# Layer 2's state-space attention: delta's product computed once per group, kept in SBUF, and the stage's instruction order rebuilt

## The chip, the cores and the metric

The kernel runs on one core of a Trainium2 chip. It is one program: five stages, one after the other, four engines that compute (TensorE, here PE; VectorE, DVE; ScalarE, ACT; GpSimd, POOL), each with its own in-order queue, and DMA queues, of which SyncE (SP) issues most. The metric is the device time of one execution in microseconds, median of several runs.

## The reference, cut to what matters

The whole network is eight residual blocks. The change touches the fifth alone, a Mamba layer on the 4096 tokens by 128 features of the activations, seen as sequences of 256 tokens. Two sequences make a group of 512 tokens; there are eight groups.

```python
xz = einsum('bld,ed->bel', hidden_states, in_proj_w)      # 128 -> 512
x, z = xz[:, :256], xz[:, 256:]
x = silu(causal depthwise conv of 4 taps over x, + conv_b)
x_dbl = einsum('bdl,kd->blk', x, x_proj_w)                # 256 -> 8 + 8 + 8
dt_lr, B, C = x_dbl split in 8, 8, 8
dt = einsum('blr,dr->bld', dt_lr, dt_proj_w)              # 8 -> 256
A = -exp(A_log) + low_rank_scale * (U @ V) / sqrt(8)
delta = softplus(dt + dt_proj_b)
def step(h, t):                                           # 256 features, 8 states
    dA = exp(dlt[..., None] * A)
    h = h * dA + (dlt * ut)[..., None] * Bt[:, None, :]
    y = einsum('bdn,bn->bd', h, Ct)
    return (h, y)
_, ys = scan(step, h0, xs)
y = (ys + u * D) * silu(z)
return einsum('bld,md->blm', y, out_proj_w)
```

Softplus is ln(1 + exp(a)). The kernel takes it as max(a, ln(1 + exp(min(a, 40)))), with a = dt + dt_proj_b, so the product dt is needed in two places: under the minimum and under the maximum.

## The kernel before, in words

**One group's way through the stage.** The group's 512 tokens are normalized (POOL, `sln`), transposed on PE and put into `ypad`; PE makes u (four shifted products against the folded convolution weights `wx`, for each of two halves of 128 features) and z; ACT takes them out of PSUM into `su` and applies SiLU. PE makes the joint projection (`ssm_xp`), ACT puts it in `sxs`, and SP sends its B and C rows to DRAM and loads B back spread over all partitions (`sB`, 1 MB each, two for a group) and C as `scc`.

Then comes delta (`ssm_dt`, `ssm_soft`). For each half c, PE multiplies `sxs` by the delta weights (`W("dt")`, in the trace `spb<-sxs,w_L2a`, 80 rows by 512 columns) into one of two PSUM banks `spb`; DVE adds the bias and takes the minimum with 40 into `s4` (in the trace `s<-spb,w_L2a`). ACT runs Exp and Ln over both halves at once (`s<-s`, 128 by 1024). PE then makes the same products a second time, and DVE, in one instruction for each half, adds the bias and takes the maximum with `s4`, into `sdl` (`sdl<-spb,w_L2a,s`). `sdl` is delta.

From delta POOL makes w = delta * u (`sw<-sdl,su`), four products of w with B (`sb<-sw,sB`, 128 by 2048, one for each half and quartet of states; seven buffers) and the spread of C (`scq<-scc,dmask`). ACT makes exp(delta * A) for one half and state at a time (`abuf<-sdl,sA`, three PSUM buffers), and DVE runs the scan (`sb<-abuf,sb`, 128 by 512), 16 of them for a group. PE transposes the scanned states in 16 steps of four into the single PSUM bank `shT`; ACT or DVE copies each out (`shs<-shT`), and PE contracts them with C (`sy<-shs,scq`). At the end ACT takes `sy` out, PE transposes back and adds u * D (`spb<-su,sdd`, `spb<-w_const,s`), DVE multiplies by the gate (`s<-spb,su`), PE applies the output projection (`spb<-w_L2a,s`), and DVE adds the result to the residual `xt`.

**What sets the order.** In this stage nothing is issued as it is written. A recorder (`Recorder`) takes down every operation of all eight groups with a due time: the step's place in a table (`SSM[2]`, entries `dt`, `soft`, `b` and so on, counted in scans), times `slot`, plus a shift for its kind (`shift`). A planner (`Recorder.run`) then goes through all of them with estimated costs, giving each free engine the ready operation with the earliest due time, and the order it finds is what each of PE, DVE, ACT, POOL is given as its queue, in order; SP is ordered too by when its transfers become ready. An operation may be marked as a choice between ACT and DVE (`rec.choice()`); `pen` is what DVE's turn costs in due time, `ahead` how far past the oldest unplanned operation it may look. A DVE operation with two inputs in SBUF, or a tensor_scalar from SBUF to SBUF, is marked `two`, and the planner starts it only when it thinks POOL is free (line 607). All instructions come out of one recording helper, line 301, so the profile tells them apart by tiles only.

**The neighbours.** The stage before is layers 0 and 1; the one behind is the expert layer, whose first loads (`w_moe`, `w_in`) wait for the end of this stage's memory. The table `SSM[4]` and the other uses of `ssm_dt` belong to a later stage with 16 states, which the change leaves as it is.

Of the kernel before, what the change touches and what calls it, by code (L numbers as in the profile page):

```python
# [16 lines left out]
AF = mybir.ActivationFunctionType  # L17
ALU = mybir.AluOpType
# [4 lines left out]
P = 128  # L23
NSEQ = 16
SEQ = 256
NTOK = NSEQ * SEQ
D = 128
GT = 512
# [646 lines left out]
class Ker:  # L675
# [565 lines left out]
    def l1(self, rec, hh, W0, F):  # L1241
# [8 lines left out]
        with ExitStack() as st:  # L1250
# [52 lines left out]
        t=((14.0, 32.0, 50.0), (14.0, 48.0, 84.0)), pen=178.7, ahead=200.0, shift={  # L1303
            "ffn": -11.8, "fin": -58.9, "front": 52.1, "gate": -15.6, "max": 39.6, "mn": -190.3, "pre": -12.5,
            "rec": 42.7, "sc": -35.2, "stick": 0.3, "tail": 116.8, "terms": 21.7, "up": 102.7, "val": 112.6, "w": 347.1,
        },
# [344 lines left out]
    def ssm_dt(self, S, c, last):  # L1651
# [11 lines left out]
        else:  # L1663
            nc.vector.tensor_scalar(ex, b, bias, 40.0, ALU.add, ALU.min)

    def ssm_soft(self, S, k):
        nc, ex, tp = self.nc, S["ex"], self.tp
        if k == 0:
            self.func(ex, ex, AF.Exp)
            self.func(ex, ex, AF.Ln, bias=1.0)  # L1670
        elif k == 1:
            S["w"] = self.ring("sw", [P, 2, GT], 2)
            nc.gpsimd.tensor_tensor(S["w"], S["dl"].rearrange("p c s t -> p c (s t)"), S["u"], ALU.mult)
        else:
            nq, cc = S["N"] // 4, S["cc"]
            cq = S["cq"] = self.ring("scq", [P, nq, 16, 32], 2)
            for q in range(0, nq, 2):
                nc.gpsimd.tensor_tensor(
                    cq[:, q : q + 2].rearrange("p q t j -> p (q t) j"),
                    cc[:, q : q + 2].rearrange("p q t -> p (q t)")[:, :, None].to_broadcast([P, 32, 32]),  # L1680
                    self.dmask[:, None, :].to_broadcast([P, 32, 32]), ALU.mult,
                )
                self.rec.also(S["w"])
# [69 lines left out]
    def ssm_out(self, S):  # L1753
# [10 lines left out]
        if S["res"]:  # L1764
# [11 lines left out]
            silu=-37.5, xp=-33, dt=(-31, -29.5, -25.5, -24), soft=(-28, -22.5, -3), bl=(-17, -9.5, -1.5, 6.5),  # L1776
            b=(-6, -2), ys=(7.2, 11.2), gt=(12, 13), out=16.3, fin=(17, 17.7, 19), slot=1.55, pen=84.3, ahead=127.7, shift={
            "": -125.5, "b": 67.9, "bload": -113.8, "dt": -200.5, "ev": 31.8, "exp": 33.9, "f": 246.7, "gt": -3.9,
            "in": 52.0, "n": -59.0, "out": 61.0, "r": -161.7, "scan": 83.0, "silu": -129.7, "soft": -121.0,
            "src": -425.4, "tr": 59.0, "xp": 3.9, "y": 118.9, "ys": -27.2,  # L1780
        },
# [1 line left out]
        2: dict(  # L1783
            nt=1, nu=4, ln=(-32, -31.5, -30), src=-29.5, u=(-28.7, -26.6), z=(-24.4, -23.4),
            silu=-22, xp=-19, dt=(-17.6, -16.7, -13.3, -12.4), soft=(-15.8, -11, 3), bl=(-17, -9.5),
            b=(-6, -2), ys=(7.2, 11.2), gt=(12, 13), out=17.5, fin=(18, 18.1, 18.2), slot=2.0, pen=111.1, ahead=183.8, shift={
            "": 112.0, "b": -43.4, "bload": -48.9, "dt": -6.2, "ev": -98.7, "exp": 66.6, "f": -14.8, "gt": -12.7,
            "in": -8.9, "n": -4.4, "out": -5.7, "scan": 2.2, "silu": -119.1, "soft": 38.6, "src": -22.5, "stick": 66.3,
            "tr": -56.2, "xp": -50.7, "y": -93.8, "ys": -93.0,
        },  # L1790
        ),
    }
# [1 line left out]
    def ssm_run(self, items, begin, norm, finish, N, after=None):  # L1794

        nq, n = N // 4, len(items)
        L = 8 * nq
        pl = self.plan
        ev = []

        def at(t, f, *a):
            ev.append((t, len(ev), f, a))

        self.rec.shift = {k: pl["slot"] * v for k, v in pl["shift"].items()}

        for i, item in enumerate(items):
            S = dict(N=N)
            o = i * L
            at(o + pl["ln"][0] - 0.01, begin, item, S)
            gens = {}  # L1810

            def step(kind, f, item, S, gens=gens):
                if kind not in gens:
                    gens[kind] = f(item, S)
                next(gens[kind], None)

            for t in pl["ln"]:
                at(o + t, step, "n", norm, item, S)
            at(o + pl["src"], self.ssm_src, S)
            if after:  # L1820
                at(o + pl["src"] + 0.1, after, item)
            for c in range(2):
                at(o + pl["u"][c], self.ssm_in, S, c)
            for k in range(2):
                at(o + pl["z"][k], self.ssm_in, S, 2 + k)
            at(o + pl["silu"], self.ssm_silu, S)
            at(o + pl["xp"], self.ssm_xp, S)
            for k in range(4):
                at(o + pl["dt"][k], self.ssm_dt, S, k % 2, k > 1)
            for k in range(3):  # L1830
                at(o + pl["soft"][k], self.ssm_soft, S, k)
            for q in range(nq):
                s = o + 8 * q
                at(o + pl["bl"][q], self.ssm_bload, S, q)
                for c in range(2):
                    at(s + 4 * c + pl["b"][0], self.ssm_b, S, q, c)
                for j in range(8):
                    at(s + j - 2.6, self.ssm_exp, S, q, j)
                    at(s + j, self.ssm_scan, S, q, j)
                    t = s + 9 + j  # L1840
                    at(t + 0.2, self.ssm_tr, S, q, j)
                    at(t + 0.5, self.ssm_ev, S, q, j)
                    if j % 2:
                        at(t + 1.3, self.ssm_y, S, q, j // 2)
            e = o + L
            for k in range(2):
                at(e + pl["ys"][k], self.ssm_ys, S, k)
                at(e + pl["gt"][k], self.ssm_gt, S, k)
            at(e + pl["out"], self.ssm_out, S)
            for t in pl["fin"]:  # L1850
                at(e + t, step, "f", finish, item, S)
        ev.sort(key=lambda e: e[:2])
        for t, _, f, a in ev:
            self.rec.key, self.rec.kind = pl["slot"] * t, f.__name__[4:] or a[0]
            f(*a)
        self.nc.record(None)
        self.rec.penalty = pl["pen"]
        self.rec.run(pl["ahead"])
        self.last_act = self.nc.scalar.last
# [248 lines left out]
    def l3_ffn(self):  # L2108
        nc = self.nc
        with ExitStack() as st:  # L2110
# [89 lines left out]
        pen=819.1, ahead=200.0, shift={  # L2200
            "aff": -5.1, "gate": -11.4, "gelu": 394.9, "hT": -62.4, "ln": 137.7, "max": -127.7, "mn": -410.9,
            "nrm": 69.1, "qkv": -128.2, "rot": -171.0, "sc": 39.2, "stick": 33.1, "tr": -158.4, "up": 14.7,
            "val": -79.2, "w": 39.8, "w2": 358.8, "wo": -262.4, "x": 1.0, "yT": 26.4,
        },
# [352 lines left out]
```

## Time and profile before

| | us |
|---|---|
| three runs | 3786.04, 3786.32, 3792.03 (median 3786.32) |
| the profiled execution | 3790.45 |
| its span, first to last instruction | 3788.6 |
| mean granted TensorE clock in it | 0.949 |
| this stage: from its first memsets to its last residual add | 871.42 to 1177.95 |
| stages before / behind | 871.42 / 2610.65 |

Over the whole span PE is busy 87%, DVE 83%, ACT 69%, POOL 65%. Within this stage's 306.53 us PE is busy 277.6, DVE 227.6, ACT 215.9 and POOL 198.8, and the granted clock is 0.97. These are sums of execution times that overlap at their edges, so an engine with 90% may have no room left.

Where POOL's eight groups begin says how the stage is paced. The instruction `sw<-sdl,su` starts at 914.8, 937.0, 961.2, 998.8, 1031.5, 1064.8, 1098.4 and 1120.8 us, so the distances are 22, 24, 38, 33, 33, 34 and 22 us: the first groups and the last follow each other closely, those in the middle are far apart.

### The profile page before, as it was taken

Reading aid. Unit: us, or ns where it says so; the run is one execution under the profiler, and the core shown is the slowest. Engines: PE = TensorE matmul, PEld = TensorE weight load, DVE = VectorE, ACT = ScalarE, POOL = GpSimd, SP = SyncE. Lnnn points to the kernel's source line nnn. Section 1 sums busy time; section 2 is a strip of 40 time slices with the busy share of each in tenths; the row PEclk is TensorE's granted clock in tenths of the full one; section 3 lists DMA queues with packets and bytes.
Section 4 is the critical chain, followed back from the end, with each engine's and each line's share of the span. In section 5 each row is a group of like instructions: output and inputs, shape, how many; then the busy total and the mean of one; then the engine's idle time right before and its main releaser. Section 6 shows DMA issues by size and latency. Waiting matters only on the chain.

```text
span 3788.6 us, 77710 instructions
## 1 busy us (share of the span) xinstructions
PE 3302.9 (87%) x31401; PEld 2222.1 (59%) x31401; DVE 3156.3 (83%) x5442; ACT 2621.7 (69%) x4276; POOL 2453.4 (65%) x1174
## 2 busy tenths in 40 slices
PE   6770168887998998799999999999999969999998
PEld 3320145563566887366666666666666647777776
DVE  4999898774886776399999999999999968888874
ACT  5660034545874333599999999999999957777765
POOL 4654323215772001699999999999999978655553
PEclk9995589998999999899999999999999989999999
DMA  1021111101111001322222222222222210000001
GB/s 48 13 38 25 37 51 36 38 21 60 69 69 38 7 6 43 107 91 92 97 97 96 98 98 92 92 97 92 92 92 93 101 60 28 11 13 6 5 18 32
DMA packets 107236, 217.94 MB, mean 58 GB/s; under 512 B 53065, under 2 KB 78284, under 8 KB 87756
## 3 DMA queue, kind: packets, MB, share of 16 engines
q1 hardware_dynamic: 104140, 208.19, 16.6%
q8 instruction: 247, 4.05, 0.5%
q10 hardware_dynamic: 2736, 4.78, 0.4%
q14 instruction: 113, 0.93, 0.1%
HBM read 182.66 MB, written 15.47 MB: 52 GB/s over the span
## 4 chain that ended last, share of the span: by engine, by line
PE 48%; ACT 17%; DVE 4%; issue 2%; POOL 1%; DMA 1%; POOLq 0%; SPq 0%; DVEq 0%; ACTq 0%
PE spb L301 14%; PE fb L301 10%; PE shT L301 8%; ACT abuf L301 5%; ACT shs L301 5%; PE gu L301 5%; PE sy L301 4%; PE md L301 3%; PE fp L301 2%; ACT L301 2%; ACT su L301 2%; ACT s L301 2%; PE mx L301 1%; DVE qr L301 1%; DVE mx L301 1%
## 5 line engine op out<-in xcount | busy, mean ns | idle before, releaser
L301 POOL TENSOR_TENSOR sb<-sw,sB 128x2048 f32<-128x2048 f32 x288 | 1338.6, 4672 | 47.2 <-PE shT L301 46.2
L301 DVE TENSOR_TENSOR_SCAN sb<-abuf,sb 128x512 f32<-128x512 f32 x1152 | 1324.9, 1209 | 43.9 <-ACT abuf L301 22.7
L301 ACT ACTIVATE abuf<-sdl,sA 128x510 f32<-128x510 f32 x1152 | 780.9, 701 | 46.8 <-DVE sb L301 42.9
L301 PEld LDWEIGHTS shT<-w_const,sb 128*128 128x128 f32 x4608 | 594.8, 194 | 284.8 <-ACT shs L301 118.3
L301 PE MATMUL shT<-w_const,sb 128*128 128x128 f32 x4608 | 667.8, 283 | 29.6 <-ACT shs L301 16.0
L301 ACT COPY shs<-shT 128x512 f32<-128x512 f32 x920 | 517.0, 596 | 50.2 <-PE shT L301 36.8
L301 PE MATMUL sy<-shs,scq 128*32 128x256 f32 x4608 | 359.9, 390 | 0.2 <-DVE shs L301 0.2
L301 PE MATMUL spb<-ypad,wx 128*128 128x512 f32 x640 | 305.9, 615 | 6.1 <-ACT su L301 3.0
L301 POOL TENSOR_TENSOR qn<-qn,qr 128x512 f32<-128x512 f32 x128 | 163.7, 1280 | 171.9 <-DVE qr L301 123.5
L301 DVE TENSOR_REDUCE mx<-fp 128x8 f32<-128x1024 f32 x160 | 193.4, 1217 | 20.0 <-PE fp L301 18.7
L301 ACT ACT_TABLE_LOAD x148 | 189.9, 1283 | 25.1 <-PE fb L301 18.3
L301 PEld LDWEIGHTS spb<-ypad,wx 128*128 128x128 f32 x640 | 116.6, 194 | 143.4 <-issue 116.2
L301 PE MATMUL gu<-my,gu 128*128 128x512 f32 x768 | 196.5, 404 | 2.6 <-ACT gu L301 2.2
L301 ACT ACTIVATE mh<-gu,w_moe 128x512 f32<-128x512 f32 x128 | 88.1, 688 | 158.4 <-PE gu L301 136.0
L301 DVE COPY shs<-shT 128x512 f32<-128x512 f32 x232 | 153.4, 685 | 46.6 <-PE shT L301 31.5
L301 PEld LDWEIGHTS sy<-shs,scq 128*32 128x32 f32 x4608 | 100.1, 108 | 113.1 <-issue 44.0
L301 ACT ACTIVATE pt<-fp 128x1024 f32<-128x1024 f32 x96 | 96.4, 1024 | 100.5 <-PE fp L301 93.8
L301 PE MATMUL fb<-wqkv_hi,hT 128*128 128x512 f32 x384 | 161.2, 438 | 4.6 <-ACT mn L301 1.4
L301 PEld LDWEIGHTS gu<-my,gu 128*128 128x128 f32 x768 | 140.3, 190 | 33.3 <-ACT gu L301 2.5
L301 POOL TENSOR_TENSOR yn<-xt,nmv 128x512 f32<-128x512 f32 x21 | 21.9, 1042 | 201.8 <-DVE nmv L301 196.1
L301 PE MATMUL spb<-sxs,w_L3a 80*128 80x512 f32 x256 | 141.2, 633 | 6.0 <-DVE s L301 2.6
L301 POOL TENSOR_TENSOR qn<-qn,nr 128x512 f32<-128x512 f32 x128 | 130.9, 1044 | 19.9 <-ACT nr L301 19.6
(385 smaller groups left out, 7063.5 us busy)
## 6 DMA issues: line engine op xcount, KB each, us to landing
sB<-scr SPq DMA_DIRECT2D x144, 1024.0 KB
QS<-qk SPq DMA_DIRECT2D x48, 128.0 KB
KS<-qk SPq DMA_DIRECT2D x48, 128.0 KB
pks<-pk SPq DMA_DIRECT2D x4, 1152.0 KB
rec<-pks SPq DMA_DIRECT2D x8, 576.0 KB
x<-xt SPq DMA_DIRECT2D x16, 256.0 KB
xo<-x SPq DMA_DIRECT2D x16, 256.0 KB
sb<-in_cw_dram SPq DMA_DIRECT2D x5, 512.0 KB
```

The costliest lines, as they stand in the source:

```text
L301: r = f(*a, **kw)
```

## The change: what it does

For the layer with 8 states (`N == 8`, this stage) the product of a half is made once. It is taken out of PSUM with the bias added, by ACT or DVE as the planner chooses, into `sdl` (`ssm_once`). The minimum with 40 is now one DVE instruction over both halves, from `sdl` into `s4`, at the head of `ssm_soft`; Exp and Ln stay; the maximum is one DVE instruction over both halves, of `sdl` and `s4` into `sdl` (`ssm_pos`). Besides, the entries `pen`, `ahead` and `shift` of this stage's plan have other values, with a new one for the maximum (`pos`), so the planner puts all of the stage in a new order.

```diff
+    def ssm_once(self, S, c):
+
+        nc, W = self.nc, S["W"]
+        if c == 0:
+            S["ex"] = self.ring("s4", [P, 2, GT], 2)
+            S["dl"] = self.ring("sdl", [P, 2, 2, SEQ], 2)
+        bias, dl = W("dtb")[:, c : c + 1], S["dl"].rearrange("p c s t -> p c (s t)")[:, c]
+        b = self.sbank()
+        self.mm(b, W("dt")[0:80, c * P : (c + 1) * P], S["xs"])
+        with self.rec.choice():
+            nc.scalar.activation(dl, b, AF.Identity, bias=bias)
+            nc.vector.tensor_scalar(dl, b, bias, None, ALU.add)
+
+    def ssm_pos(self, S):
+
+        dl = S["dl"].rearrange("p c s t -> p c (s t)")
+        self.nc.vector.tensor_tensor(dl, dl, S["ex"], ALU.max)
+
     def ssm_soft(self, S, k):
         nc, ex, tp = self.nc, S["ex"], self.tp
         if k == 0:
+            if S["N"] == 8:
+                nc.vector.tensor_scalar(ex, S["dl"].rearrange("p c s t -> p c (s t)"), 40.0, None, ALU.min)
             self.func(ex, ex, AF.Exp)
             self.func(ex, ex, AF.Ln, bias=1.0)
...
-            b=(-6, -2), ys=(7.2, 11.2), gt=(12, 13), out=17.5, fin=(18, 18.1, 18.2), slot=2.0, pen=111.1, ahead=183.8, shift={
-            "": 112.0, "b": -43.4, "bload": -48.9, "dt": -6.2, "ev": -98.7, "exp": 66.6, "f": -14.8, "gt": -12.7,
-            "in": -8.9, "n": -4.4, "out": -5.7, "scan": 2.2, "silu": -119.1, "soft": 38.6, "src": -22.5, "stick": 66.3,
-            "tr": -56.2, "xp": -50.7, "y": -93.8, "ys": -93.0,
+            b=(-6, -2), ys=(7.2, 11.2), gt=(12, 13), out=17.5, fin=(18, 18.1, 18.2), slot=2.0, pen=140.8, ahead=200.0, shift={
+            "": 158.3, "b": -31.5, "bload": -60.6, "dt": -46.9, "ev": -70.9, "exp": 14.3, "f": 41.1, "gt": -23.0,
+            "in": 10.3, "n": 9.9, "out": 62.6, "pos": -74.9, "scan": -0.6, "silu": -108.8, "soft": -34.2, "src": 0.4,
+            "stick": 14.8, "tr": -54.3, "xp": -54.0, "y": -52.9, "ys": -83.6,
...
-            for k in range(4):
-                at(o + pl["dt"][k], self.ssm_dt, S, k % 2, k > 1)
+            if N == 8:
+                for k in range(2):
+                    at(o + pl["dt"][k], self.ssm_once, S, k)
+                at(o + pl["dt"][3], self.ssm_pos, S)
+            else:
+                for k in range(4):
+                    at(o + pl["dt"][k], self.ssm_dt, S, k % 2, k > 1)
...
-            self.rec.key, self.rec.kind = pl["slot"] * t, f.__name__[4:] or a[0]
+            name = f.__name__[4:]
+            self.rec.key, self.rec.kind = pl["slot"] * t, "dt" if name == "once" else name or a[0]
```

In the built program the stage's instructions then differ so: PE has 16 products fewer (each is two matmul instructions in the trace, so 32). DVE has lost the 16 `s<-spb,w_L2a` and the 16 `sdl<-spb,w_L2a,s`, and has 3 `sdl<-spb,w_L2a` (128 by 512), 8 minima and 8 maxima (128 by 1024) and 54 instead of 50 of the copies `shs<-shT`. ACT has 13 `sdl<-spb,w_L2a` more and 74 instead of 78 of those copies. POOL and SP have the same instructions in another order. The order outside this stage is the same.

## The prediction, made before the changed kernel had run

> **What bounds the kernel now.** I read the windows of the stage first, then its instruction groups by shape, the waits, and POOL's timeline. The windows run from PE's first transpose to the first w, to the last w, to the last residual add:
>
> ```profile
> core 0: us, PE busy (x) PEld busy (x) DVE busy (x) ACT busy (x) POOL busy (x), PEclk, DMA share, GB/s
> 884.20:914.80 30.60, 28.49 (x66) 11.61 (x67) 7.24 (x36) 16.83 (x28) 7.19 (x8) 0.92 0.20 71
> 914.80:1120.80 206.00, 200.27 (x1163) 114.79 (x1162) 172.34 (x201) 169.29 (x251) 163.88 (x51) 0.99 0.20 70
> 1120.80:1177.95 57.15, 47.80 (x373) 32.32 (x372) 41.73 (x49) 26.01 (x43) 22.27 (x7) 1.00 0.04 15
> ```
>
> In the long middle PE lacks 5.7 of 206 us, DVE 33.7, POOL 42.1. So PE sets the pace, and the others wait for it. POOL's queue shows that from the other side:
>
> ```profile
> 1085.32 1.90 POOL L301 TENSOR_TENSOR scq<-scc,dmask 128x1024 f32<-128x1024 f32 x1
> 1098.43 2.36 POOL L301 TENSOR_TENSOR sw<-sdl,su 128x1024 f32<-128x1024 f32 x1 [11.21 <-DVE sdl L301]
> 1100.87 18.08 POOL L301 TENSOR_TENSOR sb<-sw,sB 128x2048 f32<-128x2048 f32 x4
> ```
>
> Here POOL stood 11.21 us until delta came, and delta came late because its second products stand in PE's full queue between transposes. The groups concerned (count | busy, mean ns | idle before):
>
> ```profile
> L301 PE MATMUL spb<-sxs,w_L2a 80*128 80x512 f32 x64 | 33.9, 615 | 0.2
> L301 DVE TENSOR_TENSOR_SCAN sb<-abuf,sb 128x512 f32<-128x512 f32 x128 | 148.0, 1206 | 9.6 <-POOL sb L301 8.4 <-ACT abuf L301 1.1
> L301 DVE SCALAR_TENSOR_TENSOR sdl<-spb,w_L2a,s 128x512 f32<-128x512 f32 x16 | 11.9, 743 | 7.0 <-PE spb L301 6.9
> L301 DVE TENSOR_SCALAR s<-spb,w_L2a 128x512 f32<-128x512 f32 x16 | 11.5, 736 | 13.3 <-PE spb L301 13.2
> L301 ACT ACTIVATE s<-s 128x1024 f32<-128x1024 f32 x16 | 16.9, 1054 | 2.5 <-DVE s L301 2.5
> ```
>
> **PE: what is removed.** 32 of the 64 matmul instructions go. One shows 615 ns, but they overlap; the chain of waits has four 512-column ones in a row at
>
> ```profile
> 1063.05 1.72 PE spb L301 x4
> ```
>
> which is 0.43 us each, so 32 x 0.43 = 13.8 us. By the same pitches (transposes 0.45 for four, 128-column products 0.107, `sy` 0.071) I summed the built orders: up to the last product for delta PE has 208.3 us of work before the change and 191.4 after; behind it 41.0 and 44.1. The sums, 249.3 and 235.5, differ by the 13.8. That all of it counts follows from the middle window; if PE were not the bound, it would be worth nothing.
>
> In the lead-in nothing is won. PE's work up to the first pair of products is 20.3 us after and 18.2 before, and the minimum, Exp, Ln and maximum follow; the second pair, which made DVE wait in 6.9 us of the rows above, is gone. I put the first w at the same 914.8.
>
> **DVE: what is exchanged.** Between the first and the last w it loses 14 x 0.736 + 14 x 0.743 = 20.7 us. It gains one take-out (0.74), seven minima and seven maxima. A 128 x 1024 tensor_tensor in SBUF took 1.22 us in the first stage (`l<-l,mx`, fastest), so seven maxima are 8.5. For a tensor_scalar of that size in SBUF there is no row: below it lies the 512-column one from PSUM with 0.736, above it the 1.22; I take 1.22, the same size and memory, so 8.5 again (5.2 by the lower). The new order also has 8 more scans in this window (1.14 each in a row, 9.1), two more copies (1.4) and one group's statistics (1.7). DVE: 172.3 - 20.7 + 0.7 + 17.0 + 9.1 + 1.4 + 1.7 = 181.5 us.
>
> The Trainium skill, "VectorE: DVE Perf Modes", section "The perf-mode tier table (the rule you actually need)", lets a float32 tensor_scalar within SBUF run at twice the rate of a tensor_tensor. By it the minimum would cost about 0.7 us, an estimate, and DVE 3.6 us less; no row of this case shows it.
>
> **DVE against POOL: the wait that is added.** The old instructions read PSUM and at most one tile of SBUF. The maximum reads two, and such an instruction did not run beside a POOL instruction:
>
> ```profile
> 179.11 4.86 POOL L301 TENSOR_TENSOR pk<-g8k,gs 128x2048 f32<-128x2048 f32 x1
> ...
> 184.05 1.75 POOL L301 TENSOR_TENSOR gs<-sg,ex 128x64 f32<-128x64 f32 x3
> ```
>
> ```profile
> 180.82 4.24 DVE L301 TENSOR_TENSOR l<-l,mx 128x1024 f32<-128x1024 f32 x1 [0.38 <-ACT mx L301]
> ```
>
> The 1.22 us of work took 4.24: it began 1.7 us into POOL's instruction and ended 1.09 after it. The wait lies inside the busy time, and scans, copies and gates queue behind it; PE's transposes wait for those scans. POOL's products here are 4.5 us each. So a minimum or maximum costs 0 to 4.5 us more.
>
> The Trainium skill, "SBUF — State Buffer", section "Who interferes with whom", speaks against the change: an exclusive lock, held for the whole instruction by whoever starts first, taken also by a tensor_scalar of the faster kind. By it the minima wait as the maxima do; were they not to, the 8 us that I allow for them next would fall away.
>
> In the new order the maximum stands right before POOL's w, which cannot start without it, so there POOL has usually nothing to run: I take 0. The minimum stands after 8 to 15 scans of the group ahead, while POOL may be in its third or fourth product: 7 minima x 1.2 us = 8 us, chosen between 0 and 32. To that 3 us of waits for PE (in this window DVE waited 19.6 us for `shT` before, but with PE full).
>
> **ACT, POOL, SP.** ACT takes 13 x 0.68 - 4 x 0.59 = 6.5 us more over a stage in which it is busy 215.9 of 306.5; hidden by its idle time, and if not, at most 6.5. POOL has the same instructions; `scq` (1.9 us) moves from behind the fourth product to between the second and third, so scans 9 to 16 can start 1.9 later. That is cover for DVE except in the last group, where it counts below. On SP one set of four small `scc` loads changes places with a 1 MB `sB` load: nothing, since no engine waits for either in the list of waits.
>
> **The sum.** By PE alone the last product for delta comes 16.9 us earlier, at about 1102.4 instead of 1119.3. It then takes the take-out 0.68, minimum 1.22, Exp and Ln 2.1, maximum 1.22, with hand-overs and a queue about 7 us, to the last w: 1109.5. By DVE the last w comes at 914.8 + 7.1 (the wait for the first product, the longest that DVE's list of waits shows for `sb`) + 181.5 + 8 + 3 = 1114.4. The later one counts. From the last w: the fourth product is ready at 22.6 (2.4 + 4 x 4.55 + 1.9, with gaps), four scans end at 27.3, and from the last scan (1152.3) to the end it took 25.65 before: 53.0 us. End: 1167.4, against 1177.95: -10.5 us. The stages behind are the same and only start earlier. The profiled run took 3790.45 with a span of 3788.6; so 3779.9 in its place. Its time lies 4.1 above the median 3786.32, and I carry the difference over: 3775.8, rounded to **3776**.
>
> **Rival 1: no change, 3785.** DVE takes PE's place. If the stalls of all 14 instructions are 1.2 us each, or only the minima's 2.4, then 17 + 3 + 7.1 + 181.5 = 208.6 puts the last w at 1123.4 and the end at 1176.4: -1.5. For it: DVE has only 13 us to spare in the window that PE alone would allow (194.7 - 181.5). Against it: the lower price of the minimum.
>
> **Rival 2: slower, 3796.** The loop through POOL: w waits for the maximum, that for Ln and Exp, these for the minimum, and the minimum for the end of POOL's products. POOL then runs nothing during the whole chain. Its own work from first to last w is 7 x 22.4 + 6.2 + 2 = 165 us. The chain is at least 1.22 + 2.1 + 1.22 + 0.4 = 4.9 us, and with the three or four scans of 1.14 that stand between minimum and maximum, partly beside Exp and Ln, 7 to 8.5. At 7.9 it gives 165 + 7 x 7.9 = 220.3, the last w at 1135.1, the end at 1188.1: +10.1. It decides from 6.4 us a group on, where 165 + 7 x 6.4 = 210 puts the end back at 1178. For it: the order has no scan of the next group to run meanwhile in the last two groups, where the maximum comes after 14 and 16 scans of the group ahead. Against it: before, POOL stood up to 11.21 us in the middle groups and the stage still was PE's.
>
> That the change leaves out less than it says is no rival: the built order has 16 products fewer.
>
> **How the numbers follow.** About 0.2% (7.6 us) is what a measurement of this kernel can tell from no change. The first case has 0.47, rival 1 0.28, rival 2 0.25. Their own spreads put about as much across the bounds each way, so faster 0.47, same 0.28, slower 0.25. The likeliest case has its own range 3770 to 3779: PE alone gives 13.8 us at most, with the cheap minimum and an earlier start 16. The whole range is 3767 to 3799, from a little past PE's full gain to rival 2 with 3 us more; I leave 1 in 10 on each side.
>
> **What would show it.** Right: 32 matmul instructions `spb<-sxs,w_L2a`; the stage ends about 10 us earlier; w starts spread more evenly, 27 to 31 us apart, the last near 1114; PE's share in the middle below 200 of 206, DVE's at 90% or more; mean of the minima 1.2 to 2.5 us, of the maxima near 1.22. Rival 1 shows maxima and minima of 2.5 us and more. Rival 2 shows POOL idle over 6 us before each w, with DVE idle too. I am wrong altogether if the first w comes several us later, if the copies out of `shT` wait longer than before though PE has less to do, or if the next stage starts later than its loads allow.

## The result: slower, and the profile after

The changed kernel took 3797.78 us (median; 3795.07 to 3802.18), the kernel before beside it 3788.16 (3786.04 to 3793.90). The ratio is 1.0021, 95% interval 1.0012 to 1.0031: 8 us slower, where 10.5 faster had been forecast. The profiled execution has a span of 3793.2 us. The stage lies in it from 869.57 (first memset) to 1184.25 (last residual add): 314.68 us against 306.53, so 8.15 longer. The loss is in this stage.

The windows of the stage after, from its start to the first w, to the last w, to the end, and the whole of it:

```profile
core 0: us, PE busy (x) PEld busy (x) DVE busy (x) ACT busy (x) POOL busy (x), PEclk, DMA share, GB/s
869.57:913.10 43.53, 29.75 (x70) 13.07 (x71) 12.82 (x71) 19.72 (x35) 12.66 (x11) 0.78 0.22 74
913.10:1129.13 216.03, 195.74 (x1145) 112.42 (x1144) 188.16 (x204) 180.55 (x273) 165.51 (x51) 0.96 0.20 71
1129.13:1184.25 55.12, 46.09 (x360) 31.26 (x358) 36.16 (x44) 20.91 (x35) 22.31 (x6) 1.00 0.00 1
869.57:1184.25 314.68, 271.59 (x1572) 156.75 (x1572) 237.15 (x319) 221.19 (x341) 200.47 (x67) 0.94 0.17 59
```

The lead-in is as long as before (43.5 against 43.4 us), the tail 2 us shorter (55.1 against 57.2). The middle took 216.0 us instead of 206.0. PE has 4.5 us less busy time there, but it lacks 20.3 us of the window instead of 5.7, and the granted clock is 0.96 instead of 0.99. (28 of the 32 instructions that went lay in this window, 12 us by the prediction's 0.43 us each. An estimate from the two clocks, 216 x 0.03 = 6.5 us, is what the lower clock gave back of that.)

The groups of the whole stage (count | busy us, mean ns | idle before, by what), first PE's transposes in the kernel before, then the changed kernel:

```profile
L301 PE MATMUL shT<-w_const,sb 128*128 128x128 f32 x512 | 81.8, 282 | 10.8 <-DVE shs L301 5.2 <-ACT shs L301 3.9 <-issue 0.7
```

```profile
L301 PE MATMUL shT<-w_const,sb 128*128 128x128 f32 x512 | 85.0, 290 | 22.9 <-DVE shs L301 14.0 <-ACT shs L301 7.9
L301 PE MATMUL spb<-sxs,w_L2a 80*128 80x512 f32 x32 | 17.6, 649 | 0.6 <-DVE sdl L301 0.4 <-ACT sxs L301 0.2
L301 DVE TENSOR_SCALAR s<-sdl 128x1024 f32<-128x1024 f32 x8 | 13.0, 1620 | 0.0
L301 DVE TENSOR_TENSOR sdl<-sdl,s 128x1024 f32<-128x1024 f32 x8 | 9.7, 1209 | 2.7 <-ACT s L301 2.7
L301 DVE TENSOR_SCALAR ln_rs<-ln_mv 128x4 f32<-128x4 f32 x2 | 6.4, 3186 | 0.0
```

The 32 matmul instructions are gone and the maxima cost what was forecast. Two rows stand out. PE's transposes stood 22.9 us, nearly all of it for the copies out of their one bank (10.8 before). And `ln_rs`, an addition on 128 x 4 elements, took 3.2 us each. That is work of the next stage, done early on groups that are finished; the stage's planner doesn't know it, and neither my prediction nor my list of the change's instructions looked at it. The kernel before has the same two instructions:

```profile
1030.32 0.17 DVE L301 TENSOR_SCALAR ln_rs<-ln_mv 128x4 f32<-128x4 f32 x1
```

Here, in its DVE timeline (start, us), it takes 0.17 us, since POOL stood idle. In the changed kernel all engines' timeline shows the second of them so:

```profile
1041.85 4.55 POOL L301 TENSOR_TENSOR sb<-sw,sB 128x2048 f32<-128x2048 f32 x1
1042.88 3.54 DVE L301 TENSOR_SCALAR ln_rs<-ln_mv 128x4 f32<-128x4 f32 x1
...
1046.34 2.33 DVE L301 TENSOR_TENSOR_SCAN sb<-abuf,sb 128x512 f32<-128x512 f32 x2
...
1048.59 0.66 DVE L301 COPY shs<-shT 128x512 f32<-128x512 f32 x1
...
1049.30 1.12 PE L301 MATMUL shT<-w_const,sb 128*128 128x128 f32 x4 [2.51 <-DVE shs L301]
```

Read it downwards. DVE starts 1.0 us into POOL's product and is done 0.02 us after that product's end (1046.40). Two scans queue behind it, then a copy out of `shT`, and for that copy PE's next four transposes stand 2.51 us. One stall on DVE has become an idle PE. Four of the eight minima (DVE's timeline) went the same way; the other four took 0.67 to 0.69:

```profile
931.18 4.76 DVE L301 TENSOR_SCALAR s<-sdl 128x1024 f32<-128x1024 f32 x1
...
962.23 1.76 DVE L301 TENSOR_SCALAR s<-sdl 128x1024 f32<-128x1024 f32 x1
...
989.05 2.51 DVE L301 TENSOR_SCALAR s<-sdl 128x1024 f32<-128x1024 f32 x1
...
1057.91 0.67 DVE L301 TENSOR_SCALAR s<-sdl 128x1024 f32<-128x1024 f32 x1
```

With 1.21 for the fourth stalled one (1021.33), the minima lost 4.76 + 1.76 + 2.51 + 1.21 - 4 x 0.67 = 7.6 us beside POOL, and the two `ln_rs` 2.83 + 3.54 - 2 x 0.17 = 6.0. The planner starts a minimum only when it thinks POOL free (line 607), but what it hands on is an order and not a time, and in the run four of the eight met POOL at work. Three windows of 6 us, columns as above:

```profile
931.10:937.10 6.00, 3.75 (x21) 1.69 (x19) 6.00 (x4) 4.13 (x7) 5.92 (x3) 0.97 0.13 51
937.10:943.10 6.00, 4.27 (x18) 2.14 (x19) 6.00 (x6) 5.76 (x10) 2.86 (x2) 0.50 0.30 124
1045.10:1051.10 6.00, 3.49 (x22) 1.78 (x20) 6.00 (x7) 2.07 (x3) 2.31 (x2) 0.86 0.15 49
```

While the 4.76 us minimum and what queued behind it held DVE, PE was busy 3.75 of 6 us (ACT stood too: its Exp waits for this minimum, and a copy out of `shT` comes behind the Exp); in the next 6 us PE was granted half its clock. The last two views are POOL's own and, for the last of its waits, DVE's:

```profile
1053.39 4.54 POOL L301 TENSOR_TENSOR sb<-sw,sB 128x2048 f32<-128x2048 f32 x1 [5.88 <-PE shT L301]
1064.25 2.36 POOL L301 TENSOR_TENSOR sw<-sdl,su 128x1024 f32<-128x1024 f32 x1 [6.31 <-DVE sdl L301]
...
1114.60 4.54 POOL L301 TENSOR_TENSOR sb<-sw,sB 128x2048 f32<-128x2048 f32 x1 [2.32 <-PE shT L301]
1129.13 2.37 POOL L301 TENSOR_TENSOR sw<-sdl,su 128x1024 f32<-128x1024 f32 x1 [9.98 <-DVE sdl L301]
```

```profile
1120.03 3.44 DVE L301 TENSOR_TENSOR_SCAN sb<-abuf,sb 128x512 f32<-128x512 f32 x3
1123.39 0.67 DVE L301 TENSOR_SCALAR s<-sdl 128x1024 f32<-128x1024 f32 x1
1123.97 1.22 DVE L301 TENSOR_TENSOR_SCAN sb<-abuf,sb 128x512 f32<-128x512 f32 x1
...
1127.83 1.22 DVE L301 TENSOR_TENSOR sdl<-sdl,s 128x1024 f32<-128x1024 f32 x1
```

POOL stood over 6 us before each w from the fifth group on, as rival 2 said. The other half of rival 2's sign is missing: DVE was not idle meanwhile. In those four waits, 29.2 us together, DVE was busy 27.3 and PE 28.4. The last minimum did not wait for POOL either: POOL's product ended at 1119.14, and DVE came to the minimum at 1123.39, after three scans.

### The profile page after: what moved, and what is told of

Read it like the earlier page. It is cut to its first block, busy times and chain, and to the rows that moved or that the text cites. A ratio compares the mean times of both kernels' runs of the same rounds, so it can differ in the third digit from the quotient of the medians.

```text
span 3793.2 us, 77636 instructions
## 1 busy us (share of the span) xinstructions
PE 3298.8 (87%) x31369; PEld 2220.8 (59%) x31369; DVE 3165.8 (83%) x5433; ACT 2627.3 (69%) x4285; POOL 2454.9 (65%) x1174
## 4 chain that ended last, share of the span: by engine, by line
PE 50%; ACT 18%; DVE 5%; issue 3%; DMA 1%; POOL 1%; POOLq 0%; SPq 0%; ACTq 0%; DVEq 0%
PE spb L301 16%; PE fb L301 11%; PE shT L301 9%; ACT abuf L301 6%; ACT shs L301 5%; PE gu L301 5%; PE sy L301 4%; PE md L301 3%; PE fp L301 2%; ACT su L301 2%; ACT L301 2%; ACT s L301 2%; DVE sb L301 1%; PE mx L301 1%; DMA sh<-xt 0%
## 5 line engine op out<-in xcount | busy, mean ns | idle before, releaser
L301 ACT ACTIVATE pt<-fp 128x1024 f32<-128x1024 f32 x96 | 96.4, 1024 | 97.4 <-PE fp L301 90.7
L301 POOL TENSOR_TENSOR yn<-xt,nmv 128x512 f32<-128x512 f32 x21 | 21.9, 1042 | 201.8 <-DVE nmv L301 193.5
L301 POOL TENSOR_TENSOR sw<-sdl,su 128x1024 f32<-128x1024 f32 x40 | 95.2, 2381 | 77.0 <-DVE sdl L301 76.8
```

Source lines behind the costliest of these rows:

```text
L301: r = f(*a, **kw)
```

## The experiments

The theories, by the letters of the expectations. P: PE bounds the stage and its saving counts in full. Q: the engines wait for one another, and it counts in part. A and R: the loop through POOL (minimum, Exp, Ln, maximum, w) bounds it. S: DVE's stalls beside POOL make PE wait. B or O: the order as such is the loss. C, D and W are told where they come. "Order held" means that the planner works on the unaltered operations and a few instructions are exchanged or dropped only as they are issued, so that every queue keeps its order. The ratios are to the kernel before, run beside them; "stage" is its length in the profiled execution (306.53 before, 314.68 after). That is one execution for each run; the stages ahead of this one, with the same instructions in all sixteen, took between 868.8 and 874.1 us in them, so a difference of two or three us in a stage says little by itself.

| run | median us | ratio, 95% interval | stage us |
|---|---|---|---|
| e1 old instructions, new plan | 3815.12 | 1.0067, 1.0054 to 1.0079 | 334.12 |
| e2 new instructions, old plan | 3823.47 | 1.0083, 1.0069 to 1.0097 | 340.92 |
| e3 products issued twice, planned anew | 3807.13 | 1.0046, 1.0033 to 1.0058 | 324.79 |
| e4 minimum from the bank | 3794.36 | 1.0014, 1.0005 to 1.0023 | 314.86 |
| e5 before, second product short, held | 3783.95 | 0.9987, 0.9978 to 0.9996 | 300.26 |
| e6 products issued twice, held | 3803.85 | 1.0040, 1.0027 to 1.0052 | 320.30 |
| e7 no minimum, held | 3791.05 | 1.0011, 1.0002 to 1.0020 | 309.98 |
| e8 w not waiting for the maximum, held | 3801.14 | 1.0036, 1.0024 to 1.0049 | 317.56 |
| e9 `ln_rs` on POOL, held | 3794.10 | 1.0010, 1.0001 to 1.0019 | 308.16 |
| e10 no minimum, `ln_rs` on POOL, held | 3789.04 | 0.9996, 0.9988 to 1.0005 | 301.27 |
| e11 minimum from the bank, `ln_rs` on POOL, new plan values | 3785.99 | 0.9990, 0.9981 to 0.9999 | 300.16 |
| e12 changed kernel, other plan values | 3783.51 | 0.9989, 0.9980 to 0.9998 | 303.35 |
| e13 minima of 8 columns, held | 3795.37 | 1.0013, 1.0004 to 1.0022 | 312.01 |
| e14 e12 with `ln_rs` on POOL | 3787.05 | 0.9995, 0.9986 to 1.0004 | 302.23 |

**The two halves of the change apart.** e1 has the old code and the new `pen`, `ahead` and `shift`; e2 the new code and the old ones.

```diff
 e1, kernel before:
-slot=2.0, pen=111.1, ahead=183.8, shift={
+slot=2.0, pen=140.8, ahead=200.0, shift={
...
 e2, changed kernel:
-slot=2.0, pen=140.8, ahead=200.0, shift={
+slot=2.0, pen=111.1, ahead=183.8, shift={
...
-"pos": -74.9
+"pos": -6.2
```

(Of `shift` the cuts here and below show single entries; most of the others change too.)

> The kernel before with the changed kernel's plan values alone: the products are still made twice, the planner only orders them by the new numbers. Theory A (the loss is the loop minimum, Exp, Ln, maximum, w, in which POOL stands about 6 us a group): the old instructions read PSUM and need not wait for POOL, so the loop is short, and the order alone costs little: within 5 us of before. Theory B (the new order itself is the loss): slower than before by 8 us or more, as the changed kernel is.

> The changed kernel with the old plan values (the maximum is given the old shift of the products, -6.2). Theory A (loop through POOL): the loop is in the instructions, not in the numbers, so it is no faster than the changed kernel, and since the numbers were not made for it rather slower: 3798 to 3815. Theory B (the new order is the loss): the old order with 13.8 us less of PE work is faster than before, 3775 to 3785.

Both are much slower than either kernel, so neither A (refuted by e1) nor B (refuted by e2) stands as it was put. A reading that fits both is that the values belong to the instructions for which they were chosen. Either half alone costs 7 or 8 thousandths, and a comparison that lets the planner run again says little about the part that was exchanged. e3 and e4 have that weakness too.

**PE's work given back, and the minimum from the bank.**

```diff
 e3, in ssm_once:
         self.mm(b, W("dt")[0:80, c * P : (c + 1) * P], S["xs"])
+        self.mm(b, W("dt")[0:80, c * P : (c + 1) * P], S["xs"])
 e4, in ssm_once, and the minimum taken out of ssm_soft:
+        nc.vector.tensor_scalar(S["ex"][:, c], b, bias, 40.0, ALU.add, ALU.min)
```

> The changed kernel, but each product of delta is issued twice in a row into the same bank, so that PE has the old amount of work again (16 products, 13.8 us). Theory A: PE is not what sets the changed kernel's time, and of the 13.8 us at most 5 show: 3798 to 3803. Theory C (PE still is the bound and the saving was really had, while something else cost 20 us): 3808 to 3812.

> The changed kernel, but the minimum is taken by halves straight from the product's bank (bias added and limited in one instruction, as before), beside the take-out into the kept tile; the product is still made once. The minimum needs no longer wait for POOL, and only the maximum stands before w. Theory A (loop through POOL): POOL's idle time before each w falls from about 6 to 2 us or so and the kernel is faster than the changed one by 10 us or more, 3775 to 3788. Theory D (DVE's amount of work is the bound): DVE has 16 x 0.736 in place of 8 x 1.6 and so about the same, 3795 to 3800.

e3 lies between its two forecasts: 9 us slower than the changed kernel. e4's stage is as long as the changed kernel's: its middle is shorter (208.3 us) and its tail longer (62.7), because more scans were left for the end (21, against 16); its two `ln_rs`, still beside POOL, took 6.8 us. Since the order moved, this decides nothing about the minimum. So from here on the order was held.

**How much PE's saving is worth.**

```diff
 e5, kernel before, as ssm_dt's second product is issued:
-        self.mm(b, W("dt")[0:80, c * P : (c + 1) * P], S["xs"])
+        self.mm(b[:, 0:8], W("dt")[0:80, c * P : (c + 1) * P], S["xs"][:, 0:8])
 e6, changed kernel, as each product is issued:
+        self.mm(b, W("dt")[0:80, c * P : (c + 1) * P], S["xs"])
         self.mm(b, W("dt")[0:80, c * P : (c + 1) * P], S["xs"])
```

> The kernel before, its order of instructions held, but the second product of delta has 8 columns in place of 512 (the rest of its bank keeps what stood there, so delta is not the reference's): PE loses about 13 us of work and nothing else changes, no instruction of DVE, ACT or POOL. Theory P (PE is the bound of the kernel before, as the prediction took it, and all of its saving counts): 11 to 13 us faster than before, ratio 0.9967. Theory Q (PE, DVE, ACT and POOL wait for one another in a fixed order, and PE's work only counts where it is the last to come): 3 to 8 us faster.

> The changed kernel with every order of instructions held, only that each product of delta is issued twice in a row (PE's old amount of work). Theory P: 12 to 14 us slower than the changed kernel, 1.0055 to 1.0060 against before. Theory Q (part of the saving had become idle time of PE in the changed kernel): 5 to 10 us slower than the changed kernel.

The windows of the two stages:

```profile
872.90:1173.16 300.26, 267.17 (x1604) 157.20 (x1604) 226.83 (x328) 215.53 (x332) 198.86 (x67) 0.97 0.18 62
```

```profile
869.85:1190.15 320.30, 280.88 (x1604) 161.25 (x1604) 234.76 (x319) 222.01 (x341) 200.42 (x67) 0.96 0.17 59
```

In the old order the stage gets 306.53 - 300.26 = 6.3 us shorter when some 13 us of PE's work go (by the pitch of the prediction; PE's busy time falls by 10.4), with no instruction of another engine altered. A few small layer-norm instructions of the next stage stand some places later in DVE's and POOL's queues; the rest of the order is that of the kernel before. In the new order the stage gets 5.6 us longer when the work comes back (PE's busy time rises by 9.3). By the ratios it is 4.9 and 7.2 us. P forecast 11 to 13 and 12 to 14; Q holds. About half of the 13 us counts. In e5's middle, PE's busy time falls by 8.4 us (200.27 to 191.84) and the window by 4.9 (to 201.15); the other 3.6 are idle time of PE, which lacks 9.3 us there against 5.7 before.

**Is it POOL?** In e8 POOL multiplies u by u for w, so that w needs nothing from DVE.

```diff
-            nc.gpsimd.tensor_tensor(S["w"], S["dl"].rearrange("p c s t -> p c (s t)"), S["u"], ALU.mult)
+            nc.gpsimd.tensor_tensor(S["w"], S["u"], S["u"], ALU.mult)
```

> The changed kernel with every order held, but POOL's w multiplies u by u in place of delta by u, so that it need not wait for the maximum (the output is not the reference's). Only POOL's wait is taken away. Theory R (loop through POOL, rival 2 of the prediction): POOL's 42 us of idle time before w are what the time is lost in, and the kernel is 10 to 25 us faster than the changed one. Theory Q or S (POOL only waits for engines that are late themselves): the scans wait for delta's Exp instead, and the kernel is within 5 us of the changed one.

It did not get faster: the ratio is 1.0036 against 1.0021, the stage 2.9 us longer. POOL no longer stands before w at all, and R's 10 to 25 us are not there. But the run is not clean, as all engines' timeline of e8 shows; the maximum now meets POOL at work:

```profile
967.48 9.99 POOL L301 TENSOR_TENSOR sb<-sw,sB 128x2048 f32<-128x2048 f32 x2
967.82 5.29 DVE L301 TENSOR_TENSOR sdl<-sdl,s 128x1024 f32<-128x1024 f32 x1
```

The eight maxima took 21.9 us in place of 9.7. That fits theory S, but 12 us more on DVE can also hide a gain, so e8 alone does not rule R out. Other runs speak against it: in e9 (below) POOL still stands 40.5 us before its eight w, against 41.8, and the stage is 6.5 us shorter; in e12 it stands 33.8 us, more than the kernel before (32.2), and the kernel is faster than that one. With what DVE does during these waits (above), POOL's standing reads as a consequence; no run cuts the loop and nothing else.

**DVE's stalls taken away, one by one.** e7 drops the minimum, e9 moves the two `ln_rs` additions to POOL, e10 does both.

```diff
 e7 and e10, as issued:
-            nc.vector.tensor_scalar(ex, dl, 40.0, None, ALU.min)
-            self.func(ex, ex, AF.Exp)
+            self.func(ex, dl, AF.Exp)
 e9 and e10, in rsqrt, for the two groups concerned:
-    nc.vector.tensor_scalar(rs, var, EPS, None, ALU.add)
+    nc.gpsimd.tensor_tensor(rs, var, self.peps.to_broadcast([P, n]), ALU.add)
```

> The changed kernel with every order held, but the minimum is left out (Exp reads the kept product; the limit at 40 is not applied): DVE loses 8 instructions with 13 us of busy time, of which some 7.5 us are waiting beside POOL's products. Theory S (DVE's stalls beside POOL make PE wait for its copies): the gap before PE's transposes at the minimum of group 1 goes and the kernel is 6 to 12 us faster than the changed one, 0.999 to 1.0005 against before. Theory R (the loop through POOL: minimum, Exp, Ln, maximum, w): each group's chain is 1 to 2 us shorter, so 8 to 12 us faster as well, with POOL idle 1 to 2 us less before every w, in the last three groups too. If neither holds: within 3 us of the changed kernel.

> The changed kernel, order held, but the two small additions ln_rs of the next stage (128x4, on DVE), which the new order puts beside POOL's products and which took 2.83 and 3.54 us there (0.17 each in the kernel before), are made by POOL just before its own ln_rs. Theory S (DVE's stalls beside POOL delay its copies, PE waits for these): PE's two waits for the copies of 2.09 and 2.51 us go; the kernel is 3 to 6 us faster than the changed one, about 1.0005 to 1.0013 against before. Theory O (only the order counts, single stalls are swallowed by slack): within 2 us of the changed kernel, 1.0016 to 1.0026.

> The changed kernel, order held, with both sources of stalls gone: the minimum is left out (Exp reads the kept product, no limit at 40) and the two ln_rs additions are on POOL. Theory S: the two gains add up, 8 to 11 us faster than the changed kernel, 0.9992 to 1.0000 against before. Theory O: no more than the minimum alone gave, 4 us.

The stages of e9 and of e10:

```profile
871.59:1179.75 308.16, 268.19 (x1572) 155.21 (x1572) 231.14 (x317) 220.97 (x341) 200.69 (x69) 0.95 0.18 61
```

```profile
869.44:1170.71 301.27, 265.11 (x1572) 153.83 (x1572) 219.02 (x309) 220.47 (x341) 199.57 (x69) 0.96 0.17 62
```

With the same PE work and the same order as the changed kernel, the stage is 6.5 us shorter in e9 and 13.4 shorter in e10; PE lacks 17.3 of e9's middle (210.40) and 13.5 of e10's (203.48), against 20.3, and its transposes stand 18.6 and 15.8 us instead of 22.9. e9 is the cleanest experiment, since hardly anything but waiting goes from DVE: two additions of four columns, 6 us of waiting, 6.5 us of stage. In time it is 1.0010 against 1.0021, about 4 us, and the two intervals overlap a little, so the time alone does not show it; e10's lies clear of the changed kernel's. S forecast 3 to 6 us for e9, 6 to 12 for e7 and 8 to 11 for e10; by the ratios it came to 4, 4 and 9.5. The gains add up, which O denied. The minimum alone was below S's range, and below the 8 to 12 of R, whose other sign failed too: POOL's last four waits before w stayed at 6.5, 6.3, 5.8 and 10.0 us.

The minimum's work and waiting go together in e7. e13 was to leave its waiting and take its work.

```diff
 e13, as issued:
-            nc.vector.tensor_scalar(ex, dl, 40.0, None, ALU.min)
+            nc.vector.tensor_scalar(ex[:, :, 0:4], dl[:, :, 0:4], 40.0, None, ALU.min)
```

> The changed kernel, order held, with minima of 2 x 4 columns in place of 2 x 512 (the rest of that tile keeps old numbers; it is zeroed once while the stage's weights are loaded). The instruction stays where it was and may still wait beside POOL's products, but its own work, 8 x 0.67 us, is nearly gone. Theory S (the waiting costs the time): the minima beside POOL still take 1 to 4 us each, and the kernel is within 2.5 us of the changed one. Theory W (the work of DVE and the length of the chain before w cost it): 4 us faster than the changed kernel or more, as without the minimum.

Its DVE timeline:

```profile
909.75 0.17 DVE L301 TENSOR_SCALAR s<-sdl 128x8 f32<-128x8 f32 x1
932.58 4.23 DVE L301 TENSOR_SCALAR s<-sdl 128x8 f32<-128x8 f32 x1
```

The same instruction took 0.17 us with POOL idle and 4.23 with POOL in a product (that one ended at 936.77, DVE at 936.81). The stage is 2.7 us shorter than the changed kernel's, and by the ratios the kernel 3 us faster, between the two forecasts and no more than the spread. Nor did the work go alone: the eight minima still took 11.2 us of DVE in place of 13.0, because the four beside POOL ended with POOL's instruction all the same and so waited longer. How the 4.7 us of e7 divide into work and waiting therefore stays open. What the profiles show is that the waiting of `ln_rs` cost about what it lasted (6.0 us, 6.5 of stage), and that 17.4 us of DVE's time in the middle, stalls and minima's work together (188.16 in the changed kernel, 170.73 in e10), cost 13.4 us of stage.

**Other plan values for the new instructions.** In e12 nothing but `pen`, `ahead` and `shift` differs from the changed kernel; they were chosen by a search in which the planner's account of costs was made to let DVE wait behind POOL. e11 has values chosen so for e4's instructions, and `ln_rs` on POOL. Both compute all of the reference. e14 is e12 with e9's edit.

```diff
 e11, e4 with e9's edit:
-slot=2.0, pen=140.8, ahead=200.0, shift={
+slot=2.0, pen=149.0, ahead=266.8, shift={
...
 e12, changed kernel:
-slot=2.0, pen=140.8, ahead=200.0, shift={
+slot=2.0, pen=49.5, ahead=276.0, shift={
...
-"dt": -46.9, "pos": -74.9, "soft": -34.2, "ev": -70.9, "tr": -54.3, "scan": -0.6
+"dt": -28.0, "pos": -269.2, "soft": 62.7, "ev": -119.2, "tr": -139.4, "scan": 68.4
```

> The product once, the minimum by halves from its bank as in the fourth run (no instruction beside POOL but the maximum), the two ln_rs additions on POOL, and plan values chosen anew for these instructions with the planner's rule book and an account of waits in order. The whole of the reference is computed. If the saving of PE work is real and the instructions' stalls and the plan were what ate it: 3 to 8 us faster than before, 0.998 to 0.9992. If what is lost lies in the product made once itself: no faster than before.

> The changed kernel with other plan values alone, chosen anew for its instructions as in the run before this one. If the changed kernel's loss is its plan: faster than the changed one by 5 us or more, 1.0008 or less against before. If it is the instructions: within 3 us of the changed kernel.

> The two remedies together: the changed kernel's instructions with the plan values of the twelfth run, and the two ln_rs additions on POOL. In the twelfth run those two took 1.73 and 1.39 us, so 2 to 3 us of stall are left to win: 0.9980 to 0.9987 against before if stalls add up also in this order, 0.9989 as in the twelfth run if this order hides them.

The windows of e12 from first to last w, and the whole stage:

```profile
916.15:1116.96 200.81, 187.66 (x1117) 107.53 (x1116) 178.53 (x192) 175.53 (x264) 166.23 (x50) 1.00 0.21 76
...
873.30:1176.65 303.35, 265.72 (x1572) 153.60 (x1572) 231.94 (x318) 220.66 (x342) 201.18 (x67) 0.97 0.17 62
```

The changed kernel's own instructions beat the kernel before by 0.0011 (0.0002 to 0.0020), some 4 us, and the changed kernel by 12, in another order. Its minima stalled once badly (4.99 us), its `ln_rs` took 1.73 and 1.39, and the granted clock in the middle is 1.00. PE's transposes still stand 20.3 us there, so that number alone does not measure the loss. e11 is as fast. e14 was to be as fast or faster; at 0.9995 it lies above both of its forecasts, and its interval reaches from their edge past no change, so whether the two remedies add up there stays open. A new search for the kernel before was not tried on the chip, so e12 shows that the instructions can win, not that they win against the best old order.

## Why the prediction was wrong

**PE's saving (-13.8, "all of it counts"): mis-sized.** The 32 instructions went. Of 13 to 13.8 us of PE's work the stage feels 5.6 to 6.3 (e5, e6). I had read "PE lacks only 5.7 of 206 us" as "PE sets the pace, and what it saves is time". But PE's queue is fixed and full of steps that wait for ACT and DVE; take work from it and it meets them earlier, as its added idle time in e5 shows. A rate of 97% says that an engine had no room, not that the others have.

**The first w: right.** 43.5 us after the stage's start, 43.4 before.

**DVE's own work from first to last w: right in sum, wrong in its parts.** Forecast 181.5 and 8 of stalls, 189.5; measured 188.16. A maximum takes 1.209 us, as forecast, and those before w did not stall. A minimum takes 0.67 where POOL is idle, not 1.22: here the Trainium skill, "VectorE: DVE Perf Modes", the perf-mode tier table, was right with its twice the rate (0.67 us against the maximum's 1.209), and my bound from the nearest row was not. Seven minima came to 12.3 us, not 16.5, and the window holds 6 scans more than before (112 against 106), not 8. Against that stand the 6.0 us that `ln_rs` lost beside POOL, which I had not counted.

**"To that 3 us of waits for PE": the step that failed.** The sum for DVE, the later of the two and so the one that counted, put the last w 243.0 us after the stage's start; it came at 259.6. The lead-in, the 7.1 us for the first product and DVE's busy time with its stalls were right within 1.4 us. The 3 us were 216.03 - 188.16 - 7.1 = 20.8: by DVE's waits 12.5 for the transposes in `shT`, 4.1 for PE's other products and 3.9 for ACT's exponentials (`abuf`). I had let DVE's waits go because PE would have less to do, and added DVE's stalls to DVE's sum alone, as if the rest of the stage went on beside them.

What the runs show in place of that is engines that wait for one another. A stall on DVE holds up copies out of `shT`, PE stands (22.9 us before its transposes instead of 10.8), the clock is lower (0.96 instead of 0.99), and then DVE waits for PE. Take the stalls and the minima away (e10), and the stage is 13.4 us shorter. But in none of the middles do DVE's waits fall to anything like 3 us. Besides the wait for the first product they are 26.6 us before, 22.4 in e5 where PE has less to do, and 25.6 in e10, where DVE is busy 17.4 us less and the window is only 12.5 shorter; even in e12 they are 15.2. So the 3 us would have failed without any stall, too. The Trainium skill, "SBUF — State Buffer", "Who interferes with whom", spoke of exactly this lock, and I drew on it for the minima and maxima only, not for the small additions of the next stage within the same window.

**ACT, POOL, SP at nothing: not tested.** ACT's busy time rose by 5.3 us (6.5 forecast). DVE's waits for `abuf` rose from 1.1 to 3.9 us in the middle, and PE's waits for ACT's copies out of `shT` from 3.9 to 7.9 in the stage. No run takes the take-outs from ACT and changes nothing else, so what they cost stays open.

**The tail: 2 us off.** 53.0 forecast from the last w on, 55.1 measured.

**The rivals.** Rival 1 took PE's place for DVE's work; DVE is busy 87% of the middle, and the end came 8 us later instead of 1.5 earlier. Rival 2 (3796) came nearest in time and had the sign and, from the fifth group on, the sight of POOL standing over 6 us. Its mechanism does not come out: DVE was busy during these waits, and by its own sum POOL's standing, 40 us before seven w or 5.7 each, is under the 6.4 from which it decides and fills 165 + 40 = 205 of the 216 us. The measured time lies inside the whole range only because that reached to rival 2, which is luck. One sign of being wrong altogether did come: the copies out of `shT` stood 64.0 us in the stage, against 58.1, though PE has less to do.

The account nearly closes: -6 for PE's work (e5, e6) and +13.4 for what e10 takes away, the minima's work included, make +7.4, where +8.15 was measured. It puts the new order itself, and ACT's added work, at nothing together; no run shows either alone.

## What to carry to other kernels

Before work is exchanged between PSUM and SBUF on DVE, list every DVE instruction that will run within SBUF alone while POOL works, those of neighbouring stages and of four columns too, and give each the rest of POOL's instruction as its price. Where the engines are all as full as here (80 to 97% of the middle) and pass work through one bank, cost a stall on one of them as a stall of all, and a saving on one at about half, as this stage showed it, until an experiment with the order held has said otherwise. Values that steer an order belong to the instructions for which they were chosen: compare two versions each with its own, or with the order held.

## What the runs showed of the hardware that was not expected

- A DVE tensor_scalar of 8 columns within SBUF, 0.15 to 0.17 us of work, took up to 4.23 us beside a POOL product (e13); one of 128 x 4 took 3.54 in the changed kernel. Both ended within 0.04 us of POOL's product, so its rest and not their own size set the wait.
- A tensor_tensor with both inputs in SBUF waits in the same way: the maximum's mean rose from 1.21 to 2.74 us when it met POOL (e8). The scans, whose one input is in PSUM and the other in SBUF, ran beside POOL in all runs at a mean of 1.20 to 1.21 us.
- After 6 us in which PE was busy 3.75, its granted clock was 0.50 for some 6 us. Over the middle of the stage the clock was 0.99 before, 0.96 after and 0.99 again without minima and `ln_rs` on DVE (e10). Not every gap has its dip: in e12 PE was busy only 1.56 us from 982 to 986, and the clock stayed at 1.00 there and in the next 6 us.
